# Soft MoE on one core: dispatch weights turned in 32-squares by VectorE, gathered in four row groups; down products of two experts in column halves; maxima spread by DRAM

## The chip, the cores and the metric

The kernel runs on one core of a Trainium2 chip. The metric is the device time of one execution in microseconds (us), lower being better. The core has five engines that run side by side: PE (TensorE, matrix products; PEld is its loading of weights), DVE (VectorE), ACT (ScalarE), POOL (GpSimd) and SP (SyncE, which issues DMAs here). SBUF is the on-chip memory, PSUM holds PE's results, DRAM is the memory off the core.

## The reference, cut to what matters

Two layers of linear attention and a soft mixture of experts, then a second block of two layers with another attention and a gated network; residuals are added after each. The change concerns the mixture alone:

```python
x = layernorm(x)                       # 8 batches, 256 tokens, 128 features
se = layernorm(slot_embeds) * scale    # 16 experts x 64 slots, 128 features
logits = einsum('bnd,esd->bnes', x, se)
dispatch = softmax(logits, axis=1)     # over the tokens
combine = softmax(logits.reshape(b, n, -1), axis=-1)   # over all 1024 slots
slots = einsum('bnd,bnes->besd', x, dispatch)
gate = gelu(einsum('besd,edf->besf', slots, Wg) + bg)
up = einsum('besd,edf->besf', slots, Wu) + bu
eout = einsum('besf,efo->beso', gate * up, Wd) + bd
return einsum('bns,bso->bno', combine, eout.reshape(b, -1, 128))
```

All of it is in fp32. The mixture runs in two layers, so 8 batches make 16 dispatches, and 16 experts make 8 pairs in each of 2 layers and 2 groups of batches, 32 pairs in all.

## The kernel before

The eight batches form two groups of four. A group goes through both mixture layers (the linear attention follows each batch's first combine), then the gated networks and the second attention. The whole program is written as steps for a planner: a step names the engines that can run it with a cost in ns each, the function that issues its instructions, and what it reads, writes and takes as buffers. The planner places steps one after another, always the one that can start earliest by its costs, with ties broken by a key that grows with PE's work; the second group's key starts 45000 later. Each engine then gets its instructions in the order of planned starts, by hand. So PE fills a wait of one group with steps of the other, and a changed cost changes the order of everything. Buffers are counted by kind (`kinds`: `comb`, `k4`, `we`, `ps` and others), and a step waits for a free one in the plan too; `ps` is PSUM's eight banks.

`dispatch(b, sl)` works on one batch. `norm` gives the rows `y` (tokens on partitions, two tiles of 128), `transposed` gives `yt`. Four steps `logits` (L511) form the logits with slots on partitions, two blocks of 128 slots each, which `evacuated` copies into `comb`. Then two paths leave `comb`.

- The dispatch softmax, by halves of four slot blocks: `greatest` (L542, DVE), `exps` (L550, ACT, into `ex`), `inverse` (L558, DVE), `divided` (L563, POOL). The result has slots on partitions, while the gather contracts over tokens, so `turn` flips it in PE, 8 flips of 128x128 a half (all flips have the line L331), each four evacuated from PSUM into `dm` (L338 on ACT or L340 on DVE). `gathered` (L584) multiplies `y` with `dm`, 512 columns at a time, and `affinely` (L416 or L418) scales the slots into `sl`.
- The combine softmax: `greater` (L528, DVE) keeps running maxima over the slot blocks, `fold` (L603, DVE) joins two halves, `turn_max` flips them (L331), `token_max` (L614, DVE) gives one maximum a token, and `spread` (L623, PE, two products with a broadcast operand) puts them on all partitions. `less` (L635, POOL) subtracts them and `exps` (L641, ACT) finishes `comb`, which is first read in `combine` (L742, PE), after the experts.

`experts(sl)` runs over 16 experts. `fetch` loads the expert's weights and its down bias into one of three `we` buffers (SP, L660 and L661). `front` makes gate and up products (L675, 256 columns: four batches of 64 slots), a gelu (L681, ACT) and the product with up (L686, DVE), giving `ht`. `back` makes the down products (L705, PE) of one expert: two batches' slots stand on 128 output partitions, and `biased` (L715, DVE) adds the bias in two instructions of 64 partitions, into the place in `sl` that the expert's slots had. For that the copies in `sl` and the embeddings `seT` have an order of halves that depends on whether the batch is odd; a third copy in `seT` (L464, POOL) serves this.

Two places elsewhere already use PE in tiles: `projected` in the second attention (L1131, four groups of 32 rows) and `products` there (L1223, four groups of 32 columns). L1027, L1030 and L958 are the gated network's products; L972 is a DVE addition there of a 128x512 PSUM tile and an SBUF tile.

Of the kernel before, what the change touches and what calls it, by code (L numbers as in the profile page):

```python
# [13 lines left out]
P = 128  # L14
# [162 lines left out]
def macaron_kernel(ctx: ExitStack, tc: tile.TileContext, i: dict, out: bass.AP):  # L177
# [27 lines left out]
        "comb": (NJ * N, 9),  # L205
        "slots": (NJ * NB * 4 * S1, G),
        "k4": (1024, 6),
# [3 lines left out]
        "we": (6 * P + D, 3),  # L211
# [98 lines left out]
    seT = const.tile([P, NJ, 3, S], F32, tag="seT", name="seT")  # L310
# [11 lines left out]
    def mms(*columns):  # L322
        return sum(2 * max(107, 0.84 * n) for n in columns)
# [24 lines left out]
    def normalized(tiles, twice=False):  # L348
# [21 lines left out]
        step({"DVE": 400 * n}, stats, [t[2] for t in tiles], [mv], takes=[t[3] for t in tiles])  # L370
        step({"POOL": 600 + 160 * n}, root, [mv], [mv])
        for t, (dst, src, r, w) in enumerate(tiles):
            def apply(e, t=t, dst=dst, src=src):
                (nc.gpsimd if e == "POOL" else nc.vector).tensor_scalar(  # L374
                    dst(), src(), mv.ap[:, 2 * t : 2 * t + 1], mv.ap[:, 2 * t + 1 : 2 * t + 2],
                    ALU.subtract, ALU.mult,
                )

            step({"POOL": 800, "DVE": 360}, apply, [r, mv], [w])
# [31 lines left out]
    def affinely(dst, src, r, w, n):  # L411
# [8 lines left out]
        step({"ACT": act(n, True), "DVE": dve(n, 120)}, run, [*r, "ng"], w)  # L420


    def keys():
# [8 lines left out]
        for h in range(2):  # L432
# [17 lines left out]
            def finish(e, pse=pse, part=part):  # L450
                if e == "ACT":
                    nc.scalar.activation(
                        seT[:, part, 0:2], pse.ap, AF.Identity, bias=bs, scale=gs
                    )
                else:
                    nc.vector.tensor_scalar(
                        seT[:, part, 0:2], pse.ap, gs, bs, ALU.mult, ALU.add
                    )
# [3 lines left out]

            def again(_, part=part):
                nc.gpsimd.tensor_copy(seT[:, part, 2], seT[:, part, 0])  # L464

            step({"POOL": 400}, again, cells, [("seT2", j) for j in js])
# [25 lines left out]

    def dispatch(b, sl):


        odd, q = b % 2, b % BG
        y = norm(b, True)
        yt = transposed(y, TT, True)
        comb = Buf("comb", (P, NJ, N))
        pm = Buf("k2", (P, 2, N))
        for u in range(4):
            pl = ps_(2, N)

            def logits(_, u=u, pl=pl):
                for j in range(2):  # L510
                    mm(  # L511
                        pl.ap[:, j, :],
                        seT[:, 2 * u + j, odd : odd + 2].rearrange("p k s -> p (k s)"),
# [5 lines left out]
                [yt, *((k, 2 * u + j) for j in range(2) for k in ("seT", "seT2"))], [pl],  # L519
                takes=[(comb, u), pm],  # L520
# [5 lines left out]
            if u:  # L526
                def greater(_, u=u, pl=pl):
                    nc.vector.tensor_tensor(  # L528
                        pm.ap, pl.ap, comb.ap[:, 0:2, :] if u == 1 else pm.ap, ALU.max
                    )  # L530

                step({"DVE": dve(2 * N)}, greater, [pl, pm, (comb, 0)], [pm])


        for h in range(2):
            mx = Buf("sm", (P, 16))
            ex = Buf("k4", (P, 4, N))
            dm = Buf("k4", (P, TT, 4 * P))
            half = [(comb, 2 * h), (comb, 2 * h + 1)]

            def greatest(_, h=h, mx=mx):
                nc.vector.tensor_reduce(  # L542
                    mx.ap[:, 0:4], comb.ap[:, 4 * h : 4 * h + 4, :], AX.X, ALU.max, negate=True
# [4 lines left out]
            def exps(_, h=h, mx=mx, ex=ex):  # L548
                for j in range(4):
                    nc.scalar.activation(  # L550
                        ex.ap[:, j, :], comb.ap[:, 4 * h + j, :], AF.Exp,
# [3 lines left out]
            step({"ACT": 2200}, exps, [*half, mx], [mx, ex], [dm], table="exp")  # L555
# [6 lines left out]
            def divided(_, mx=mx, ex=ex):  # L562
                nc.gpsimd.tensor_tensor(  # L563
                    ex.ap, ex.ap, mx.ap[:, 8:12].unsqueeze(2).to_broadcast([P, 4, N]), ALU.mult
                )

            step({"POOL": 1950}, divided, [mx, ex], [ex])
            for t in range(TT):
                pt = ps_(4, P)

                def turn(_, t=t, pt=pt, ex=ex):
                    for j in range(4):
                        flip(pt.ap[:, j, :], ex.ap[:, j, ts(t, P)])

                step({"PE": flips(4)}, turn, [ex], [pt], takes=[dm])
                evacuated(
                    lambda t=t, dm=dm: dm.ap[:, t, :],
                    lambda pt=pt: pt.ap.rearrange("p j c -> p (j c)"), [pt], [(dm, t)], 4 * P,
                )
            po = ps_(4, 2, S)  # L580

            def gathered(_, dm=dm, po=po):
                for t in range(TT):
                    mm(  # L584
                        po.ap.rearrange("p j k s -> p (j k s)"), y.ap[:, t, :], dm.ap[:, t, :],
                        start=(t == 0), stop=(t == TT - 1),
                    )

            step(
                {"PE": mms(512, 512)}, gathered,  # L590
                [(y, t) for t in range(TT)] + [(dm, t) for t in range(TT)], [po],
            )


            blocks = slice(1, 3) if odd else slice(0, 4, 3)
            affinely(
                lambda h=h: sl.ap[:, 4 * h : 4 * h + 4, q // 2, blocks, 0:S],
                lambda po=po: po.ap, [po], [(sl, j, q) for j in range(4 * h, 4 * h + 4)], 512,
            )


        def fold(_):
            nc.vector.tensor_tensor(pm.ap[:, 0], pm.ap[:, 0], pm.ap[:, 1], ALU.max)  # L603

        step({"DVE": dve(2 * N)}, fold, [pm], [pm])
# [3 lines left out]
        def turn_max(_):  # L609
            for t in range(TT):  # L610
                flip(pt.ap[:, t, :], pm.ap[:, 0, ts(t, P)])
# [6 lines left out]
        pb = ps_(N)  # L618
        mb = Buf("k1", (P, N))

        def spread(_):
            for t in range(TT):
                mm(  # L623
                    pb.ap[:, ts(t, P)], mn.ap[:, t : t + 1].to_broadcast([P, P]), ident,
                    start=True, stop=True,
                )

        step({"PE": mms(P, P)}, spread, [mn], [pb], takes=[mb])
        evacuated(lambda: mb.ap, lambda: pb.ap, [pb], [mb], N)
# [17 lines left out]
    def experts(sl):  # L647
        def whole(j):
            return [(sl, j, q) for q in range(BG)]

        def eo():
            return sl.ap.rearrange("p j a k s -> p j (a k s)").rearrange(
# [3 lines left out]
        def fetch(e):  # L656
            we = Buf("we", (P, 6 * P + D))

            def run(_):
                nc.sync.dma_start(we.ap[:, 0 : 6 * P], i["We"][e])  # L660
                nc.sync.dma_start(we.ap[:, 6 * P :], i["bd"][e].partition_broadcast(P))  # L661

            step({"SP": 1000}, run, [(sl, 0, BG - 2)], [we])
            return we

        def front(e, we):
            j, k = e // 2, e % 2
            ht = Buf("k2", (P, 2, BG * S))
            for c in range(2):
# [3 lines left out]
                def hidden(_, c=c, pe=pe):  # L673
                    for m in range(2):
                        mm(  # L675
                            pe.ap[:, m, :], we.ap[:, ts(2 * m + c, P)],
                            sl.ap[:, j, :, k::2, 0:S], start=True, stop=True,
# [7 lines left out]
                def up(_, c=c, pe=pe, ga=ga):  # L685
# [6 lines left out]
                    {"PE": mms(256, 256)}, hidden, [we, *whole(j)], [pe], takes=[ga, (ht, c)]  # L692
# [5 lines left out]
        def back(e, we, ht):  # L698
            j, k = e // 2, e % 2
            po = ps_(NB, P)  # L700

            def down(_):
                for q in range(NB):
                    for c in range(2):
                        mm(  # L705
                            po.ap[:, q, :], ht.ap[:, c, ts(q, P)], we.ap[:, ts(4 + c, P)],
                            start=(c == 0), stop=(c == 1),
                        )

            step({"PE": mms(*[P] * 2 * NB)}, down, [we, (ht, 0), (ht, 1)], [po])  # L710

            def biased(_):
                for u in range(2):
                    rows = slice(u * S, (u + 1) * S)
                    nc.vector.tensor_tensor(  # L715
                        eo()[rows, j, (u ^ k) :: 2, 0:D], po.ap[rows],
# [624 lines left out]
```

## Time and profile before

| what | value |
|---|---|
| median of 3 runs | 789.29 us (788.82 to 789.86) |
| profiled execution, its own time | 788.46 us |
| its span | 786.8 us |
| PE busy | 759.1 us, 96% |
| DVE busy | 536.7 us, 68% |
| ACT busy | 458.3 us, 58% |
| POOL busy | 340.6 us, 43% |
| DMA, mean over the span | 47 GB/s |

Busy times come from one profiled execution. The span is from its first to its last instruction; the execution's own time is 1.7 us longer. A group of instructions is shown as its line, engine and operation, what it writes and reads by the program's names, its shape and its count, then busy time, mean ns of one, and after the second bar the engine's idle time before them with what ended it. A single fp32 product shows as two records, a flip as one. A record's duration is longer than the distance from one record to the next[...]; distances are read from the order of time.

### The profile page before, as it was taken

To read this page: it belongs to the slowest core of one execution; us is meant where nothing else is said; L and a number is where in the kernel's file an instruction comes from. 1 tells how busy PE (TensorE), PEld (TensorE's weight loads), DVE (VectorE), ACT (ScalarE), POOL (GpSimd) and SP (SyncE) were. 2 spreads that over 40 slices of the span, in tenths; PEclk is the share of its full clock that TensorE was granted. 3 is DMA by queue.
4 is the path that set the end of the run, shared out by engine and by line. 5 is a ranking of instruction groups with operands and counts; after the bars stand their busy time and mean duration, and the time that the engine had idled before them with its cause. 6 is when DMAs were issued, how large, how long until landed. Compare 5 with 4: busy or idle time off the path is not lost.

```text
span 786.8 us, 12435 instructions
## 1 busy us (share of the span) xinstructions
PE 759.1 (96%) x4584; PEld 630.9 (80%) x4584; DVE 536.7 (68%) x1170; ACT 458.3 (58%) x826; POOL 340.6 (43%) x365
## 2 busy tenths in 40 slices
PE   3899999999999999999999999999999999999997
PEld 2667787999887888878888987898787987778875
DVE  5899787478886887895664455447897488873242
ACT  2889889555894689895363324426475255633232
POOL 7998424323367545547722042234544323620001
PEclk9999999999999999999999999999999999999999
DMA  6101233313230122332523100000000000000000
GB/s 192 40 0 39 77 97 95 112 54 114 74 95 1 55 66 76 94 106 58 153 74 92 47 1 1 1 0 2 1 1 1 1 1 15 2 0 1 21 7 15
DMA packets 27580, 36.96 MB, mean 47 GB/s; under 512 B 3808, under 2 KB 18816, under 8 KB 27520
## 3 DMA queue, kind: packets, MB, share of 16 engines
q1 hardware_dynamic: 25968, 35.62, 15.4%
q8 instruction: 36, 0.59, 0.3%
q10 hardware_dynamic: 1488, 0.53, 0.3%
q14 instruction: 24, 0.20, 0.1%
q0 software_dynamic: 64, 0.03, 0.0%
HBM read 35.12 MB, written 1.05 MB: 46 GB/s over the span
## 4 chain that ended last, share of the span: by engine, by line
PE 87%; DVE 5%; POOL 4%; DMA 1%; issue 1%; ACT 1%; ACTq 0%; POOLq 0%; SPq 0%; DVEq 0%
PE ps L958 24%; PE ps L675 13%; PE ps L742 7%; PE ps L705 7%; PE ps L331 5%; PE ps L511 5%; PE ps L584 5%; PE ps L1030 4%; PE ps L1055 3%; PE ps L1027 3%; PE ps L1192 2%; POOL k L563 1%; PE ps L1131 1%; PE ps L1117 1%; PE ps L1223 1%; POOL sm L368 1%
## 5 line engine op out<-in xcount | busy, mean ns | idle before, releaser
L675 PE MATMUL ps<-slots,we 128*128 128x256 f32 x512 | 124.4, 380 | 0.0
L338 ACT COPY k<-ps 128x512 f32<-128x512 f32 (+1 forms) x97 | 50.5, 540 | 122.1 <-PE ps L958 74.3
L675 PEld LDWEIGHTS ps<-slots,we 128*128 128x128 f32 x512 | 93.0, 189 | 17.6 <-issue 6.0
L958 PE MATMUL ps<-comb,comb 128*128 128x256 f32 x448 | 104.6, 381 | 2.5 <-ACT k L338 1.7
L958 PE MATMUL ps<-comb,slots 128*128 128x256 f32 x448 | 103.4, 379 | 0.0
L563 POOL TENSOR_TENSOR k<-k,sm 128x1024 f32<-128x1024 f32 x32 | 61.0, 1908 | 85.8 <-DVE sm L558 85.7
L958 PEld LDWEIGHTS ps<-comb,comb 128*128 128x128 f32 x448 | 83.3, 190 | 16.2 <-ACT k L338 2.7
L958 PEld LDWEIGHTS ps<-comb,slots 128*128 128x128 f32 x448 | 83.9, 190 | 14.3 <-issue 3.6
L635 POOL TENSOR_TENSOR comb<-comb,k 128x1024 f32<-128x1024 f32 x32 | 75.8, 2386 | 19.4 <-DVE k L340 14.1
L681 ACT ACTIVATE k<-ps,bg 128x256 f32<-128x256 f32 x128 | 55.3, 473 | 41.3 <-PE ps L675 36.2
L331 PE MATMUL ps<-ident,k 128*128 128x128 f32 x408 | 61.7, 279 | 16.5 <-POOL k L374 9.1
L686 DVE SCALAR_TENSOR_TENSOR k<-ps,bu,k 128x256 f32<-128x256 f32 x128 | 56.9, 477 | 25.1 <-ACT k L681 24.2
L972 DVE TENSOR_TENSOR comb<-ps,k 128x512 f32<-128x512 f32 x48 | 33.0, 688 | 59.5 <-ACT k L338 30.1
L331 PEld LDWEIGHTS ps<-ident,k 128*128 128x128 f32 x408 | 48.8, 143 | 28.6 <-POOL k L374 10.9
L705 PEld LDWEIGHTS ps<-we,k 128*128 128x128 f32 x512 | 65.0, 191 | 7.5 <-issue 3.4
L715 DVE TENSOR_TENSOR slots<-ps,we 64x256 f32<-64x256 f32 x128 | 53.7, 420 | 25.0 <-PE ps L705 20.0
L705 PE MATMUL ps<-we,k 128*128 128x128 f32 x512 | 67.6, 275 | 0.8 <-DVE k L686 0.8
L550 ACT ACTIVATE k<-comb,sm 128x256 f32<-128x256 f32 x128 | 63.4, 498 | 5.8 <-DVE sm L542 3.4
L943 POOL TENSOR_TENSOR comb<-comb 128x512 f32<-128x512 f32 x16 | 25.1, 1570 | 92.8 <-ACT comb L980 56.2
L511 PE MATMUL ps<-k,seT 128*128 128x256 f32 x256 | 62.7, 384 | 0.7 <-ACT k L416 0.7
L742 PEld LDWEIGHTS ps<-slots,comb 128*128 128x128 f32 x512 | 59.6, 192 | 3.0 <-issue 2.6
L742 PE MATMUL ps<-slots,comb 128*128 128x129 f32 x512 | 60.8, 275 | 0.0
(143 smaller groups left out, 1413.1 us busy)
## 6 DMA issues: line engine op xcount, KB each, us to landing
we<-in_We SPq DMA_DIRECT2D x64, 384.0 KB, 3.1
we<-in_bd SPq DMA_DIRECT2D x64, 64.0 KB, 3.0
x<-in_L_attn_x SPq DMA_DIRECT2D x4, 256.0 KB, 5.9
comb<-in_h2T SPq DMA_DIRECT2D x4, 256.0 KB, 4.6
slots<-in_h1T SPq DMA_DIRECT2D x4, 256.0 KB, 6.3
out<-x SPq DMA_DIRECT2D x8, 128.0 KB, 1.7
k<-in_slot_embeds ACTq DMA_DIRECT2D x2, 256.0 KB, 6.1
k<-in_hs SPq DMA_DIRECT2D x2, 256.0 KB, 3.5
```

The costliest lines, as they stand in the source:

```text
L331: nc.tensor.transpose(po, src, ident)
L511: mm(pl.ap[:, j, :], seT[:, 2 * u + j, odd : odd + 2].rearrange("p k s -> p (k s)"), yt.ap, start=True, stop=True,)
L550: nc.scalar.activation(ex.ap[:, j, :], comb.ap[:, 4 * h + j, :], AF.Exp, bias=mx.ap[:, j : j + 1], accum_out=mx.ap[:, 4 + j : 5 + j],)
L563: nc.gpsimd.tensor_tensor(ex.ap, ex.ap, mx.ap[:, 8:12].unsqueeze(2).to_broadcast([P, 4, N]), ALU.mult)
L635: nc.gpsimd.tensor_tensor(raw, raw, mb.ap.unsqueeze(1).to_broadcast([P, 4, N]), ALU.subtract)
L675: mm(pe.ap[:, m, :], we.ap[:, ts(2 * m + c, P)], sl.ap[:, j, :, k::2, 0:S], start=True, stop=True,)
L681: nc.scalar.activation(ga.ap, pe.ap[:, 0, :], AF.Gelu, bias=bg[:, e, c : c + 1])
L686: nc.vector.scalar_tensor_tensor(ht.ap[:, c, :], pe.ap[:, 1, :], bu[:, e, c : c + 1], ga.ap, ALU.add, ALU.mult,)
L705: mm(po.ap[:, q, :], ht.ap[:, c, ts(q, P)], we.ap[:, ts(4 + c, P)], start=(c == 0), stop=(c == 1),)
L715: nc.vector.tensor_tensor(eo()[rows, j, (u ^ k) :: 2, 0:D], po.ap[rows], we.ap[rows, 6 * P :].unsqueeze(1).to_broadcast([S, NB, D]), ALU.add,)
L742: mm(po.ap[:, t, 0 : D + 1], comb.ap[:, j, ts(t, P)], eo()[:, j, q, 0 : D + 1], start=(j == 0), stop=(j == NJ - 1),)
L958: mm(bank.ap[:, o], w(k)[:, c, ts(o, P)], rhs().rearrange("p (c n) -> p c n", c=2)[:, c, :], start=(start and o + c == 0), stop=(stop and ...
```

## The change

- Dispatch weights: `turn` is now a DVE transpose of 128x1024 a half, in place, which turns every square of 32x32 by itself. Slots of a square stand on its 32 columns and 32 tokens on its partitions; each group of 32 partitions then holds 32 of every 128 slots, for all 256 tokens in eight chunks. `ex` is now one buffer of kind `comb` for both halves; `dm` and its evacuations are gone.
- Rows: each group of 32 partitions needs all tokens, so `replicated` writes `y` to DRAM in four DMAs and reads it back in four, once for each group of partitions, as `yr`.
- Gather: for each of eight chunks four products of 32 rows and 256 columns, one in each row group of PE, each into its own PSUM bank; then four affine copies of 256 columns.
- Maxima: `largest` is one DVE reduction of 128x2048 over the slot blocks (its eight neighbours lie 256 elements apart). `spread` on PE becomes a DMA of the two columns of maxima to DRAM and one that reads them back to all partitions.
- Experts: `back` does a pair. Each expert's down product has 64 columns of weights and goes to one column half of PE, and so to 64 of the output's partitions; one DVE addition of 128x512 adds the bias. The odd and even orders of halves, and the third copy in `seT`, are gone. The pair's two weight buffers are held to the end of its down product.
- Buffers: `comb` 9 to 10, `k4` 6 to 4, `we` 3 to 4.
- The planner's costs of several steps are set anew.

```diff
-        "comb": (NJ * N, 9),
+        "comb": (NJ * N, 10),
-        "k4": (1024, 6),
+        "k4": (1024, 4),
-        "we": (6 * P + D, 3),
+        "we": (6 * P + D, 4),
...
-        return sum(2 * max(107, 0.84 * n) for n in columns)
+        return sum(2 * max(112, 0.84 * n) for n in columns)
...
-        step({"DVE": 400 * n}, stats, [t[2] for t in tiles], [mv], takes=[t[3] for t in tiles])
+        step({"DVE": 455 * n}, stats, [t[2] for t in tiles], [mv], takes=[t[3] for t in tiles])
-            step({"POOL": 800, "DVE": 360}, apply, [r, mv], [w])
+            step({"POOL": 840, "DVE": 430}, apply, [r, mv], [w])
-        step({"ACT": act(n, True), "DVE": dve(n, 120)}, run, [*r, "ng"], w)
+        step({"ACT": act(n, True) + 90, "DVE": dve(n, 120)}, run, [*r, "ng"], w)
...
+        def spill(_):
+            for k in range(4):
+                nc.sync.dma_start(
+                    spilled[b].rearrange("i (t k) d -> i k t d", k=4)[:, k],
+                    y.ap[32 * k : 32 * k + 32],
+                )
+        def spread(_):
+            for a in range(4):
+                nc.sync.dma_start(yr.ap[32 * a : 32 * a + 32], spilled[b])
+        step({"SP": 1800}, spill, [(y, t) for t in range(TT)], [("y", b)])
+        step({"SP": 1800}, spread, [("y", b)], [yr])
...
-                    nc.vector.tensor_tensor(
-                        pm.ap, pl.ap, comb.ap[:, 0:2, :] if u == 1 else pm.ap, ALU.max
-                    )
...
-                def turn(_, t=t, pt=pt, ex=ex):
-                    for j in range(4):
-                        flip(pt.ap[:, j, :], ex.ap[:, j, ts(t, P)])
...
+                nc.vector.transpose(
+                    ex.ap[:, part].rearrange("p j n -> p (j n)"),
+                    ex.ap[:, part].rearrange("p j n -> p (j n)"),
+                )
+            step({"DVE": 1200}, turn, [(ex, h)], [(ex, h)])
...
-                for t in range(TT):
-                    mm(
-                        po.ap.rearrange("p j k s -> p (j k s)"), y.ap[:, t, :], dm.ap[:, t, :],
-                        start=(t == 0), stop=(t == TT - 1),
-                    )
+            for c in range(N // 32):
+                for a, po in enumerate(pos):
+                    rows = slice(32 * a, 32 * a + 32)
+                    mm(
+                        po.ap, yr.ap[rows, c, :], ex.ap[rows, :, 32 * c : 32 * c + 32],
+                        start=(c == 0), stop=(c == N // 32 - 1), tile_position=(32 * a, 0),
+                    )
+        step({"PE": 3600}, gathered, [yr, (ex, 0), (ex, 1)], pos)
...
-            nc.vector.tensor_tensor(pm.ap[:, 0], pm.ap[:, 0], pm.ap[:, 1], ALU.max)
+            nc.vector.tensor_reduce(
+                pm.ap, comb.ap.rearrange("p j n -> p n j"), AX.X, ALU.max
+            )
...
-                mm(
-                    pb.ap[:, ts(t, P)], mn.ap[:, t : t + 1].to_broadcast([P, P]), ident,
-                    start=True, stop=True,
-                )
+            nc.sync.dma_start(maxima[b].rearrange("t p -> p t"), mn.ap)
+            nc.sync.dma_start(
+                mb.ap, maxima[b].rearrange("t p -> (t p)").partition_broadcast(P)
+            )
...
-            step({"SP": 1000}, run, [(sl, 0, BG - 2)], [we])
+            step({"SP": 1000}, run, [(sl, "in", BG - 2, 0)], [we])
...
-                    {"PE": mms(256, 256)}, hidden, [we, *whole(j)], [pe], takes=[ga, (ht, c)]
+                    {"PE": mms(256, 256)}, hidden, [we, *whole(j), *filled], [pe], takes=[ga, (ht, c)]
...
-                        mm(
-                            po.ap[:, q, :], ht.ap[:, c, ts(q, P)], we.ap[:, ts(4 + c, P)],
-                            start=(c == 0), stop=(c == 1),
-                        )
+                        for k in range(2):
+                            mm(
+                                po.ap[S * k : S * k + S, q, :], hts[k].ap[:, c, ts(q, S)],
+                                wes[k].ap[:, ts(4 + c, P)], start=(c == 0), stop=(c == 1),
+                                tile_position=(0, S * k),
+                            )
...
-                        eo()[rows, j, (u ^ k) :: 2, 0:D], po.ap[rows],
-                        we.ap[rows, 6 * P :].unsqueeze(1).to_broadcast([S, NB, D]), ALU.add,
+                    eo()[:, j, :, 0:D], po.ap,
+                    wes[0].ap[:, 6 * P :].unsqueeze(1).to_broadcast([P, BG, D]), ALU.add,
...
-            if e >= 1:
-                back(e - 1, *got.pop(e - 1))
+            if e % 2 == 0 and e:
+                back(e // 2 - 1, *zip(*got[e - 2 : e]))
+        back(NJ - 1, *zip(*got[E - 2 :]))
...
-        step({"DVE": 500}, blocks, [pkv], [kv])
+        step({"DVE": 730}, blocks, [pkv], [kv])
...
-            step({"POOL": 1200, "DVE": 800}, run, r, w)
+            step({"POOL": 1450, "DVE": 950}, run, r, w)
```

## The prediction

> **What bounds the kernel now.** I read the page's busy shares, then the chain that ended last, then a table of stretches, then the costliest groups, and last the order of TensorE's work in two short windows.
>
> ```profile
> PE 759.1 (96%) x4584; PEld 630.9 (80%) x4584; DVE 536.7 (68%) x1170; ACT 458.3 (58%) x826; POOL 340.6 (43%) x365
> PE 87%; DVE 5%; POOL 4%; DMA 1%; issue 1%; ACT 1%; ACTq 0%; POOLq 0%; SPq 0%; DVEq 0%
> ```
>
> PE is busy for 96% of the span and carries 87% of the chain. A busy PE needn't be a full one, so I look at start distances: in the order of PE's work a 128-column record starts 0.11 us after the one before it, a 256-column one after 0.216, a 512-column one after 0.43. All records times these distances make 743 us of 786.8. PE's own work sets the time.
>
> ```profile
> 15.00:66.00 51.00, 47.27 (x228) 35.15 (x229) 45.78 (x86) 43.40 (x118) 50.32 (x42) 1.00 0.09 29
> 66.00:200.00 134.00, 132.47 (x822) 114.51 (x821) 102.41 (x248) 98.98 (x175) 52.70 (x63) 1.00 0.30 87
> 200.00:350.00 150.00, 147.93 (x896) 125.05 (x895) 122.56 (x276) 121.92 (x255) 79.64 (x74) 1.00 0.24 71
> 400.00:787.00 387.00, 379.49 (x2330) 313.75 (x2329) 228.66 (x450) 165.32 (x236) 111.05 (x122) 1.00 0.04 13
> ```
>
> Columns: stretch, length, busy time of PE, PEld, DVE, ACT, POOL, clock, DMA share, GB/s. From 66 us on PE alone is full. The opening (15 to 66, before the first expert) is different: POOL is busy 50.3 of 51 us, DVE 45.8, ACT 43.4. There a shorter PE buys nothing by itself.
>
> ```profile
> L331 PE MATMUL ps<-ident,k 128*128 128x128 f32 x408 | 61.7, 279 | 16.5 <-POOL k L374 9.1 <-DVE k L374 4.3 <-POOL k L563 1.9
> L584 PE MATMUL ps<-k,k 128*128 128x512 f32 x128 | 60.3, 593 | 0.0
> L705 PE MATMUL ps<-we,k 128*128 128x128 f32 x512 | 67.6, 275 | 0.8 <-DVE k L686 0.8
> L623 PE MATMUL ps<-ident,sm 128*128 128x128 f32 x64 | 9.8, 276 | 0.4 <-DVE sm L614 0.4
> ```
>
> These are the PE groups that the edit touches: flips, the gather of slots, the down products, the spreading of maxima.[...]
>
> ```profile
> 38.56 1.04 PE L331 MATMUL ps<-ident,k 128*128 128x128 f32 x8
> 39.44 1.89 PE L511 MATMUL ps<-k,seT 128*128 128x256 f32 x8
> ...
> 553.06 1.02 PE L1027 MATMUL ps<-k,w1T 128*128 128x512 f32 x2
> 554.01 1.07 PE L1223 MATMUL ps<-k,kv 128*32 128x256 f32 x16
> 555.01 1.12 PE L1030 MATMUL ps<-k,w2T 128*128 128x512 f32 x2
> ```
>
> Start, length, group. Eight flips take 39.44 - 38.56 = 0.88 us, 0.110 each. L1223 is an existing product on four column tiles: 16 records of 256 columns in 1.00 us, where one after another they would take 16 x 0.216 = 3.46. So tiles do run side by side, four at a time.
>
> [...]L1223 gets 3.46/1.00, and L1131 (four row groups, 32 records of 128 columns) takes 1.10 us where 3.6 would be serial. [...]L1027's two records need 0.86 us but L1223 starts 0.95 after them, and its own four rounds of 0.216 last 1.00, so a burst pays about 0.09 on the way in and 0.13 inside and out, 0.22; L1131's, by the same count, 0.3.
>
> **PE, part by part.** There are 16 dispatches (8 batches, 2 layers) and 32 expert pairs.
> - Flips of dispatch weights go: 16 x 16 x 0.110 = 28.2 us off.
> - The spread by PE goes: 64 records x 0.112 = 7.2 off.
> - Gather: before, 128 records x 0.43 = 55.0. After, 8 chunks x 4 row groups of 256 columns, two records each: 16 rounds x 0.216 = 3.46 a dispatch, 55.3 in all. Four row groups only make up for contracting 32 rows at a time. Plus 16 bursts x 0.22 = 3.5.
> - Down products: before, 512 x 0.112 = 57.3. After, twice the products with half the columns of weights, two tiles side by side: 16 rounds x 0.112 a pair, again 57.3. Plus 32 bursts x 0.25 (between the two measured) = 8.0.
>
> Sum: -28.2 - 7.2 + 0.3 + 3.5 + 8.0 = **-23.6 us** of PE time.
>
> **What the opening gives back.** In 15 to 66 us some 60 of those flips and all of 16 spread records run: 6.6 + 1.8 = 8.4 us, less about 0.8 for three or four new bursts, 7.6. POOL's two passes a half (L563 1.91, L635 2.39 us) stay, so POOL, DVE and ACT keep the opening at its length and PE waits there. I count **+7.6**. It could be 0: the subtraction L635 (19.3 us of POOL in the opening) will come later, behind the DMAs, so that L563 goes first and the experts may start sooner. Late next would be DVE.
>
> **VectorE.** Removed: running maxima L528 32.7 us (21.7 + 11.0), L603 12.6, the 128 bias adds L715 53.7, and about half of 64 evacuations of flipped weights, 19. Added: 32 transposes of 128x1024. None is in the trace;[...] I take L542, a pass over the same 128x1024, 1.21 us: 39 us; twice that is the upper end[...]. 16 maxima over a view whose neighbours lie 1 KB apart: 2.2 us if like L542,[...] 35 is the lower end. 32 bias adds of 128x512 by L972's 0.69: 22. Affine copies: 64 of 256 columns in place of 32 of 512 (0.53 against 0.81 on DVE, 0.56 against 0.78 on ACT): up to +10, on either.[...] DVE's 537 us has 250 to spare; from 66 us on PE hides all of it. In the opening the same counts leave DVE and ACT about where they are. ACT loses some 18 us of evacuations.
>
> **Waits and queues.** The rows y go to DRAM and come back four times over: eight DMAs, two landings of about 3 us (We lands in 3.1). In the first dispatch the gather starts 13 us after y, so 6 us are hidden. Maxima: two DMAs, 2.9 us as norm_g's 128 single words and 3.0 as the broadcast bo, in place of 0.85 us on PE and ACT. L635 waits for that, and behind it only L641 and the combine at L742, first at 146 us while the dispatches' L635 end near 84: 60 us of cover. All ten DMAs join SP, in front of weight fetches: each dispatch holds SP for two landings. SP already waits 215 us for L705 to free weight buffers, so it is idle time that they fill; bounds 0 to 32 x 2 us, taken 0. The weights of two experts are now held until the pair's down product; a fetch then has only the next expert's 1.8 us of PE in front of it against 3.1 us to land: 1.3 us short, 28 times. Before, the same sum is 3.1 against 1.8 + 0.9, 0.4 short, and PE shows no wait for it: the other group's work fills it. Taken 0, bound 36. Two fewer copies on POOL (L464): 0.8, under the opening's start. The gather now takes four PSUM banks and starts for all eight slot blocks at once, so the first expert waits for whole dispatches, not halves: inside the opening's +7.6. Bias DMAs are as many and half as large: 0.
>
> The new planner costs reorder everything. PE lies idle 12.1 us in all after 66 us; a better order saves at most that, a worse one may double it. I take 0.
>
> **Sum.** -23.6 + 7.6 = -16.0 on an execution of 788.46 us (span 786.8 and 1.7 around it); the median shown is 0.8 above it: 789.29 - 16 = **773 us**.
>
> **Rivals.**
> - The whole PE gain arrives, because the experts start sooner: 766; with half of the idle time planned away, 760. For it: L635 leaves the head of POOL's queue. Against: DVE is busy 90% of the opening. Chance 0.22.
> - Slower: the weights of pairs. If the 28 short fetches, with SP held by landings in front of them (up to 2 us more), are not filled by the other group, each costs 1.3 to 2 us: up to 36 to 56 us, 809 at 36. It decides from 16 us of stall, 0.6 us a pair. Against: PE is full from 66 us on with a similar shortage now. With half of it, 791. Chance 0.16.
> - In between, some of that stall: 780 to 789, chance 0.09, of which 0.04 is no change.
> - The tiles don't do what they say: half-width column tiles run one after another, +57 us, 830. L1223 with quarter tiles speaks against it. Chance 0.02, inside the slower ones.
>
> **Numbers.** The forecast, 769 to 779, has 0.53. Faster by over 0.2% (1.6 us, about what a measurement here can tell) 0.80; within 0.04; slower 0.16. Range 757 (whole gain and most idle time) to 794 (a bit over half of the fetch stall).
>
> **What would show it.** Right: L331's records drop by 256 to 152 plus the 64 others, L623 is gone, gather records of 256 columns start in fours 0.216 us apart, down records in pairs 0.11 apart; PE's idle time grows by about 8 us before the first expert and not after. Wrong: waits of PE for DMA into we, a first expert well away from 66 us, transposes over 2 us that make DVE the releaser of PE, or down records that start singly.

## The result, and the profile after

The changed kernel takes **909.2 us** (904.2 to 910.5, four runs) against 789.1 for the kernel before: the ratio is 1.151 [1.147, 1.156]. I had forecast 773. The profiled execution took 910.47 us, span 908.8, so the two spans differ by 122.0 us.

I read the same views again, first the busy shares and the chain that ended last.

```profile
PE 776.4 (85%) x5672; PEld 646.5 (71%) x5672; DVE 526.1 (58%) x1018; ACT 441.0 (49%) x808; POOL 342.1 (38%) x365
PE 61%; DMA 19%; POOL 7%; DVE 6%; ACT 3%; issue 3%; SPq 1%; ACTq 0%; POOLq 0%
```

PE carries 61% of the chain where it carried 87%, and DMA 19% where it had 1%. PE's idle time (span less busy) grew from 27.7 to 132.4 us, by 104.7; its busy time grew by 17.3. Together that is the 122.0. Then the stretches, with the columns of before:

```profile
15.00:66.00 51.00, 31.82 (x220) 26.26 (x221) 35.33 (x49) 26.51 (x78) 26.62 (x27) 0.80 0.53 77
66.00:200.00 134.00, 95.67 (x836) 78.61 (x838) 73.01 (x108) 76.38 (x154) 53.36 (x37) 0.86 0.31 84
200.00:350.00 150.00, 122.90 (x1048) 108.76 (x1040) 93.40 (x195) 76.62 (x157) 53.20 (x63) 0.92 0.22 67
...
500.00:909.00 409.00, 401.00 (x2532) 326.87 (x2531) 223.62 (x442) 179.26 (x256) 130.61 (x142) 1.00 0.05 16
```

No engine is full in any of the first three stretches, which have the dispatches: in the first, PE is busy 31.8 of 51 us, POOL 26.6 (50.3 before). So no single engine's work sets the time there, and the chain names DMAs. From 500 us on, where no dispatch is left, PE is full as before. The granted clock (third column from the right) falls to 0.80; it was 1.00 everywhere. In this trace it is 1.00 or 0.50 at any moment, and the column is the mean over the stretch. The first expert starts at 102.3 us, where it started at 65.6: with PE's waits for weights below, that makes two of the signs of being wrong that the prediction had named.

The groups that the edit touched:

```profile
L596 PE MATMUL ps<-comb,k 32*128 32x256 f32 x1024 | 67.5, 416 | 17.5 <-ACT k L416 12.5 <-ACT comb L562 3.1 <-DVE sm L775 1.3
L724 PE MATMUL ps<-we,k 128*64 128x128 f32 x1024 | 66.7, 283 | 4.7 <-DVE k L704 4.7
L612 DVE TENSOR_REDUCE k<-comb 128x256 f32<-128x2048 f32 x16 | 58.9, 3679 | 0.0
L583 DVE STREAM_TRANSPOSE comb<-comb 128x1024 f32<-128x1024 f32 x32 | 39.4, 1236 | 48.6 <-POOL comb L575 47.9
L646 POOL TENSOR_TENSOR comb<-comb,k 128x1024 f32<-128x1024 f32 x32 | 74.5, 2350 | 135.9 <-DMA k<-m 131.3
L331 PE MATMUL ps<-ident,k 128*128 128x128 f32 x152 | 28.7, 296 | 38.3 <-DVE k L612 17.8 <-POOL k L374 11.5 <-ACT slots L416 5.0
```

The transposes cost 1.236 us each (1.21 estimated, as L542), the strided maxima 3.68 (2.2 if like L542). L646 is the subtraction of the maxima. In the kernel before it was this:

```profile
L635 POOL TENSOR_TENSOR comb<-comb,k 128x1024 f32<-128x1024 f32 x32 | 75.8, 2386 | 19.4 <-DVE k L340 14.1 <-ACT k L338 5.2
```

Each pass is as long as ever (2.35 us for 2.39), but POOL now stands idle 131.3 us in front of it for the maxima's read. Two bursts in the order of PE's work show the tiles:

```profile
278.17 3.73 PE L596 MATMUL ps<-comb,k 32*128 32x256 f32 x64
...
291.63 2.02 PE L724 MATMUL ps<-we,k 128*64 128x128 f32 x32
293.58 1.13 PE L693 MATMUL ps<-slots,we 128*128 128x256 f32 x4
```

A gather burst has 64 records of 256 columns: 13.8 us one after another, 3.7 here. A pair's down burst has 32 of 128 columns: 3.6 us one after another, 293.58 - 291.63 = 1.95 here. Tiles run four and two at a time, as forecast.

Now the queue that issues the DMAs. L632 is the store of the maxima, L635 their read:

```profile
78.98 0.38 SPq L632 DMA_DIRECT2D m<-sm  x1
88.31 0.34 SPq L635 DMA_DIRECT2D k<-m  x1
89.04 0.37 SPq L632 DMA_DIRECT2D m<-sm  x1
99.22 0.33 SPq L635 DMA_DIRECT2D k<-m  x1
104.90 0.37 SPq L632 DMA_DIRECT2D m<-sm  x1
113.79 0.32 SPq L635 DMA_DIRECT2D k<-m  x1
114.20 3.53 SPq L673 DMA_DIRECT2D we<-in_We  x2
```

These lines stand one after another. In 35 us SP issues three stores of 1 KB and their three reads and nothing else, in the order of its program: each read waits for its store to land, and comes 9.0, 9.8 and 8.5 us after the store's issue has ended. The weights (L673) come after that. The DMA issues of the page (KB each, median us from issue to landing), and the waits (us in total, times, longest):

```profile
we<-in_We SPq DMA_DIRECT2D x64, 384.0 KB, 4.4
y<-k SPq DMA_DIRECT2D x64, 32.0 KB, 1.9
k<-m SPq DMA_DIRECT2D x16, 128.0 KB, 4.8
...
m<-sm SPq DMA_DIRECT2D x16, 1.0 KB, 9.1
```

```profile
POOL comb L646 <- DMA k<-m: 131.3, 14, 17.8
PE ps L693 <- DMA we<-in_We: 25.9, 11, 6.0
PE ps L763 <- POOL slots L744: 24.1, 4, 10.3
SPq L635 <- DMA m<-sm: 108.6, 15, 9.8
```

The store of 1 KB takes 9.1 us to land, a store of 32 KB of rows 1.9. SP stands 108.6 us for it in 15 waits. PE waits for weights, and for a memset (L744) that is behind the subtraction on POOL (one at 194.3 us stands behind a subtraction that waited until 186.0 for its maxima). How POOL's order carries the wait on, from its timeline (the bracket is idle time before the group):

```profile
32.12 1.59 POOL L374 TENSOR_SCALAR k<-x,sm 128x128 f32<-128x128 f32 x2
48.67 4.65 POOL L646 TENSOR_TENSOR comb<-comb,k 128x1024 f32<-128x1024 f32 x2 [14.96 <-DMA k<-m]
53.28 5.59 POOL L575 TENSOR_TENSOR comb<-comb,sm 128x1024 f32<-128x1024 f32 x3
```

POOL stands 15 us and then has three divisions of dispatch weights (L575) to catch up. The turns on DVE (L583, 47.9 us of idle time behind L575) and the gather after them wait for those.

### The profile page after: what moved, and what is told of

Same layout as the page of the kernel before. It is cut to its first block, busy times and chain, and to the rows that moved or that the text cites. A ratio compares the mean times of both kernels' runs of the same rounds, so it can differ in the third digit from the quotient of the medians.

```text
span 908.8 us, 14628 instructions
## 1 busy us (share of the span) xinstructions
PE 776.4 (85%) x5672; PEld 646.5 (71%) x5672; DVE 526.1 (58%) x1018; ACT 441.0 (49%) x808; POOL 342.1 (38%) x365
## 4 chain that ended last, share of the span: by engine, by line
PE 61%; DMA 19%; POOL 7%; DVE 6%; ACT 3%; issue 3%; SPq 1%; ACTq 0%; POOLq 0%
PE ps L979 21%; PE ps L693 10%; DMA m<-sm 8%; PE ps L724 5%; DMA k<-m 5%; DMA we<-in_We 4%; POOL comb L646 4%; PE ps L763 4%; PE ps L1076 3%; PE ps L1051 3%; PE ps L1048 3%; PE ps L528 2%; PE ps L331 2%; DVE k L612 2%; PE ps L1213 2%
## 5 line engine op out<-in xcount | busy, mean ns | idle before, releaser
L693 PE MATMUL ps<-slots,we 128*128 128x256 f32 x512 | 134.5, 407 | 27.6 <-DMA we<-in_We 25.9
L646 POOL TENSOR_TENSOR comb<-comb,k 128x1024 f32<-128x1024 f32 x32 | 74.5, 2350 | 135.9 <-DMA k<-m 131.3
L763 PE MATMUL ps<-slots,comb 128*128 128x129 f32 x512 | 68.8, 292 | 24.1 <-POOL slots L744 24.1
L338 ACT COPY k<-ps 128x512 f32<-128x512 f32 (+1 forms) x63 | 32.9, 528 | 115.1 <-PE ps L979 71.8
L652 ACT ACTIVATE comb<-comb 128x1024 f32<-128x1024 f32 x32 | 33.8, 1055 | 103.4 <-POOL comb L646 98.3
L575 POOL TENSOR_TENSOR comb<-comb,sm 128x1024 f32<-128x1024 f32 x32 | 60.2, 1895 | 62.0 <-DVE sm L570 62.0
L704 DVE SCALAR_TENSOR_TENSOR k<-ps,bu,k 128x256 f32<-128x256 f32 x128 | 57.5, 476 | 44.0 <-ACT k L699 43.7
L596 PE MATMUL ps<-comb,k 32*128 32x256 f32 x1024 | 67.5, 416 | 17.5 <-ACT k L416 12.5
L596 PEld LDWEIGHTS ps<-comb,k 32*128 32x128 f32 x1024 | 57.8, 207 | 25.3 <-ACT comb L338 12.7
L724 PE MATMUL ps<-we,k 128*64 128x128 f32 x1024 | 66.7, 283 | 4.7 <-DVE k L704 4.7
L724 PEld LDWEIGHTS ps<-we,k 128*64 128x64 f32 x1024 | 58.2, 141 | 15.8 <-DVE k L704 7.1
L583 DVE STREAM_TRANSPOSE comb<-comb 128x1024 f32<-128x1024 f32 x32 | 39.4, 1236 | 48.6 <-POOL comb L575 47.9
```

The lines of the kernel that those rows point to most:

```text
L575: nc.gpsimd.tensor_tensor(ex.ap[:, part], ex.ap[:, part], mx.ap[:, 8:12].unsqueeze(2).to_broadcast([P, 4, N]), ALU.mult,)
L583: nc.vector.transpose(ex.ap[:, part].rearrange("p j n -> p (j n)"), ex.ap[:, part].rearrange("p j n -> p (j n)"),)
L596: mm(po.ap, yr.ap[rows, c, :], ex.ap[rows, :, 32 * c : 32 * c + 32], start=(c == 0), stop=(c == N // 32 - 1), tile_position=(32 * a, 0),)
L646: nc.gpsimd.tensor_tensor(raw, raw, mb.ap.unsqueeze(1).to_broadcast([P, 4, N]), ALU.subtract)
L652: nc.scalar.activation(raw, raw, AF.Exp)
L693: mm(pe.ap[:, m, :], we.ap[:, ts(2 * m + c, P)], sl.ap[:, j, k, :, 0:S], start=True, stop=True,)
```

## The experiments

Theory A: the stores of the maxima, by SP and POOL standing in order behind them, make the 120 us. Rivals: the pairs of experts (B), the dispatch part (B2), the strided maxima on DVE (C), the new planner costs.

**The maxima's way: PE again, and DMAs alone.** In the changed kernel, the maxima are spread by PE as before:

```diff
-        step({"SP": 450}, spill, [mn], [("max", b)])
-        step({"SP": 450}, spread, [("max", b)], [mb])
+        step({"PE": mms(P, P)}, spread, [mn], [pb], takes=[mb])
+        evacuated(lambda: mb.ap, lambda: pb.ap, [pb], [mb], N)
```

> The changed kernel, with the maxima spread by two PE products and an evacuation again, as before the change; all else is the changed kernel. Theory A (the two DMAs of the maxima, 9.1 and 4.8 us to landing where the plan counts 2.65 each, hold SP's and POOL's queues in order): the loss goes, and the PE sum of the prediction shows: 789 - 23.6 + 7.2 + 7.6 = 780, at most 790. Theory B (the weights of pairs held longer, rows by eight DMAs and the four-bank gather make the loss): 870 or more.

Measured: 812.2 us, ratio to before 1.031 [1.028, 1.034]. 97 us of the 120 are gone. It is not the 780 expected, so something else costs too. The opening and the next stretch of this run:

```profile
15.00:66.00 51.00, 43.65 (x328) 37.07 (x330) 46.54 (x60) 39.58 (x114) 45.12 (x36) 0.93 0.41 116
66.00:200.00 134.00, 124.09 (x1117) 106.24 (x1113) 93.72 (x178) 83.91 (x152) 49.78 (x54) 0.97 0.27 85
```

All engines are back at work, still short of before (47.3 and 132.5 of PE). The counterpart is the kernel before with nothing but the two DMAs in place of PE's spread:

> The kernel before, with one part of the change alone: maxima spread by the two DMAs in place of two PE products and an evacuation. Theory A: much slower, 840 to 900, with POOL waiting for the reading DMA by over 80 us in all. Theory B: within 2% of before, 780 to 800.

Measured: 889.5 us, 1.128 [1.126, 1.129], 101 us slower, with no rows through DRAM, no tiles and no pairs. Its store lands in 9.1 us as well, and POOL waits 122.5 us for the read. A holds in both directions.

**Is it the form of the store?** The changed kernel, with the two columns of maxima flipped by PE into two rows first, so that the store writes two rows of 512 B in place of 256 single words:

```diff
+            flip(prow.ap[0:TT, :], mn.ap)
...
+            nc.vector.tensor_copy(mrow.ap[0:TT, :], prow.ap[0:TT, :])
...
-            nc.sync.dma_start(maxima[b].rearrange("t p -> p t"), mn.ap)
+            nc.sync.dma_start(maxima[b], mrow.ap[0:TT, :])
```

> The changed kernel; the maxima (two words on each of 128 partitions) are first flipped by PE to two rows of 128 words and copied by DVE, so that the store to DRAM is two runs of 512 B and not 256 single words; the reading DMA is unchanged. Theory A1 (single words stored to DRAM are what takes 9 us): the store lands in 2 to 2.5 us, as the rows y do (1.9), and the time falls to 775 to 795. Theory A2 (any way through DRAM that the queues wait for costs it): the store still lands late, or the time stays over 850.

Measured: 833.6 us, 1.057 [1.054, 1.060]: 76 us less than the changed kernel, though not the 775 to 795 expected. The waits:

```profile
POOL comb L656 <- DMA k<-m: 75.1, 13, 17.6
SPq L643 <- DMA m<-k: 10.3, 10, 2.0
```

SP's wait for the store falls from 108.6 us to 10.3: between the end of a store's issue and its read lie 7.1 to 10.2 us with single words, and with rows SP never stands longer than 2.0 for a store. POOL still waits 75 us for the read, which comes in SP's turn; yet the time is only 21 us above that of the kernel with PE's spread, so a total of waits is not a price.

**Is it the plan?** The planner had been told 0.45 us for each of the two DMAs and a lag of 2.2 us for all DMAs (from a step's end until its successor may start). With lags by the trace:

```diff
-            s.ready = max((n.end + self.LAG[n.engine] for n in s.needs), default=0)
+            s.ready = max((n.end + getattr(n, "lag", self.LAG[n.engine]) for n in s.needs), default=0)
...
-        step({"SP": 450}, spill, [mn], [("max", b)])
-        step({"SP": 450}, spread, [("max", b)], [mb])
+        step({"SP": 450}, spill, [mn], [("max", b)]).lag = 8700
+        step({"SP": 450}, spread, [("max", b)], [mb]).lag = 4400
```

> The changed kernel with the same instructions; the planner alone is told that the store of the maxima takes 8.7 us from its issue until its successor may start, and the reading DMA 4.4, where it counted 2.2 for both. Theory A-plan (the queues are put in an order that the real times don't fit, and would do no harm in a fitting one): most of the loss goes, 775 to 810. Theory A-wait (SP standing at the landing is the loss whatever the order): over 870.

Measured: 859.6 us, 1.092 [1.087, 1.097], between the two. A plan that knows the delay wins back 50 us: it puts other work ahead of the subtraction, and POOL's wait for the read falls from 131.3 to 43.9 us. It doesn't take the stores off SP: they take 11.7 us to land here, and PE waits 38.5 us for weights.

**SP or POOL?** The same stores and reads, but nobody waits for them on POOL:

```diff
-                    raw, raw, mb.ap.unsqueeze(1).to_broadcast([P, 4, N]), ALU.subtract
+                    raw.rearrange("p j (t c) -> p (j t) c", c=P),
+                    raw.rearrange("p j (t c) -> p (j t) c", c=P),
+                    ident.unsqueeze(1).to_broadcast([P, 4 * TT, P]), ALU.subtract,
...
-            step({"POOL": 2400}, less, [mb, *half], half)
+            step({"POOL": 2400}, less, half, half)
```

> The changed kernel with both DMAs of the maxima still issued on SP, in the same form, but nobody reads what they bring: the subtraction on POOL takes the identity in place of the maxima (same shape and engine, and the exponent a scale of 0.125, so the combine weights are not the reference's) and waits for no DMA. The changed kernel with the maxima on PE took 812 us, 97 less than the changed kernel. Theory POOL: the 97 us come from POOL standing in order behind the subtraction that waits for the maxima (131 us of waits). Then this run falls to 800 to 830. Theory SP: they come from the 9.1 us stores that hold SP, so that rows and weights are fetched late. Then it stays at 870 or above, with PE's waits for the DMA into we at some 26 us as before. In between, both.

Measured: 866.5 us, 1.099 [1.096, 1.102], between the ranges of the two theories, so both have a share. Of the 97 us 43 go with POOL's wait, 54 stay with the stores on SP. The split is rough, since the plan's order moves with the edit, and the two are not independent: PE's wait for weights grows to 49.8 us here. Waits of this run:

```profile
PE ps L695 <- DMA we<-in_We: 49.8, 10, 18.1
...
SPq L635 <- DMA m<-sm: 105.2, 14, 9.3
```

SP stands as long as in the changed kernel (108.6 there); the weights of the experts come up to 18 us late, and PE waits for them.

**The strided maxima (C).** Running maxima of the kernel before in place of L612, in the kernel with PE's spread:

> The changed kernel with the maxima spread by PE (812 us in the run before) and, on top, with the running maxima and the fold of the kernel before in place of the one strided reduction of 128x2048, which takes 3.68 us where the plan counts 2.30. Theory C (that reduction stands on DVE in front of the work that PE waits for): 12 us or more faster than 812. Theory B (weights of pairs, rows through DRAM): no more than 5 us faster.

Measured: 822.8 us, 1.043 [1.042, 1.045], 10 us more than with the strided reduction. C falls.

**The new costs.** The kernel before with only the planner's six changed costs:

> The kernel before with the new planner costs alone: the same instructions in another order. The prediction took 0 for this, with 12 us of PE's idle time as the bound: 782 to 801. If the new costs fit the chip better, as their sizes suggest (128 columns 112 against 107 ns, statistics 455 against 400), 782 to 788; a theory that the new order itself makes the rest of the loss: 800 or more.

Measured: 791.9 us, 1.0039 [1.0024, 1.0054]: 3 us.

**The experts alone.** The kernel before with pairs, column halves, the order of `sl` and four weight buffers:

> The kernel before with the experts' part of the change alone: down products of two experts in column halves, one bias addition for both, four weight buffers, the plain order of halves; dispatch, maxima and planner costs are those of before. By the burst times of the run before (1.90 us a pair against 1.79) PE's sum gives 788.5 + 32 x 0.2 = 795 if nothing waits. Theory B1 (the weights of a pair held longer are what costs): 805 to 825, with PE waiting for DMA into we. Against B1: 788 to 797.

Measured: 809.7 us, 1.026 [1.025, 1.028], 21 us. The time lies in the range of the theory, but PE waits for weights only 3.5 us in all, so the stall that I had made the slower rival is not there. To part holding from tiles, this run has full-width products, but holds two experts' weights and puts their `back` steps together:

```diff
-            if e >= 1:
-                back(e - 1, *got.pop(e - 1))
+            if e % 2 == 0 and e:
+                back(e - 2, *got.pop(e - 2))
+                back(e - 1, *got.pop(e - 1))
```

> The kernel before with one thing of the pairs: four weight buffers (and 12 for 14 of the smallest temporaries, to make room), and the down products and bias adds of two experts issued together after both fronts, still full width, one expert after the other, without tiles. The pairs alone cost 21 us. Theory hold: the price is in holding the weights of two experts and in the order that this makes: 800 to 806, PE's busy time as before. Theory tiles: the price is in the tiles themselves, in the 32 bursts[...]: 787 to 792.

Measured: 797.5 us, 1.011 [1.010, 1.013], between the two: 9 us for holding. The bursts make 32 x 0.20 = 6.4. No run tells the last 6 of 21 apart. In the trace of the experts alone PE is idle 7 us longer than before (808.1 - 773.3 = 34.8 us for 27.7), and the mean granted clock is 0.994, which costs at most 808.1 x 0.006 = 4.8 (an estimate); with the bursts that is 18 of the 21.

**The dispatch part alone.** DVE's turns, rows through DRAM and the gather in row groups, with PE's spread, running maxima and the old experts and costs:

> The kernel before with the dispatch part of the change alone: weights turned by VectorE, rows through DRAM, gather in four row groups; maxima (running, spread by PE), experts and planner costs are those of before. PE's sum: 788.5 - 27.9 + 16 x 0.33 = 766, and 773 with the opening's give-back of the prediction. Theory B2 (rows through DRAM and the four-bank gather cost it): 785 to 805. Against B2: 764 to 777.

Measured: 792.4 us, 1.0047 [1.0031, 1.0063]. PE's sum for this part is 28.2 less 0.3 and some 5 for 16 bursts, near 23 us, so 766; 26 us are given back. Two of its stretches, with the columns of before:

```profile
15.00:66.00 51.00, 42.52 (x260) 33.37 (x259) 45.83 (x78) 40.29 (x117) 45.95 (x42) 0.87 0.22 61
...
200.00:350.00 150.00, 141.41 (x1128) 126.21 (x1127) 125.65 (x284) 110.84 (x241) 77.67 (x77) 0.99 0.33 93
```

I took the opening for the place, and kept PE's flips in its four dispatches (with `comb` and `k4` at the 9 and 6 of before, and the planner's offset of the second group at 52 us):

> The kernel before with the dispatch weights turned by VectorE and gathered in four row groups in 12 of the 16 dispatches; the first four, those of the opening, keep PE's flips and its gather of 512 columns. The planner's offset of the second half of the batches is 52 us in place of 45. The 12 spare PE 12 x (1.76 - 0.33) = 17 us. Theory opening: what all sixteen gained (23 us of PE) was given back in the opening, which DVE, POOL and ACT bound; with the opening left alone 774 to 783, stretch 15 to 66 as before with PE busy about 47 us and at a full clock. Rival: a turned dispatch gives its gain back wherever it stands, by DVE's turns, the rows' way through DRAM and the order: 787 to 796.

Measured: 798.9 us, 1.012 [1.010, 1.014], above both ranges. Its stretches:

```profile
15.00:66.00 51.00, 48.77 (x233) 37.13 (x234) 46.72 (x88) 43.59 (x116) 50.32 (x43) 1.00 0.21 55
...
200.00:350.00 150.00, 138.05 (x1100) 123.13 (x1099) 131.25 (x277) 108.38 (x231) 72.94 (x72) 0.98 0.32 90
```

The opening is whole again, and yet PE is busy 138 us in 200 to 350 where it was busy 148 before. So the opening is not the only place; as offset and buffers moved too, this run can't say what the opening alone is worth. Another offset for all sixteen:

> All sixteen dispatches turned by VectorE and gathered in row groups, nothing else of the change, as in the run that took 792.4 us, but with the planner's offset of the second half of the batches at 48 us in place of 45. Theory order: the gain of 23 us of PE was lost to an unlucky order, which the offset moves: 780 to 786. Theory opening: the opening takes it back under any such order: 789 to 796, with PE busy 42 to 44 us in 15 to 66 at a low clock.

Measured: 789.8 us, 1.0010 [0.9998, 1.0022], no difference from before. This other order doesn't bring the gain, and the result lies in the range of the opening's theory, with the signs named for it: PE is busy 42.5 of 51 us in 15 to 66, at a clock of 0.90. Then I took one suspect at a time, with the order of all engines kept. Without the DVE transposes:

> The dispatch part alone (792.4 us) with its 32 DVE transposes left out, so that the slots are gathered with wrong weights; their place in the plan and its cost stay, so the order of every engine is the same. 39 us of DVE are gone. Theory turns: the 22 us that PE saves are lost because DVE's turns stand in front of the gather and of DVE's other work: 772 to 782. Theory rows: little, 789 to 793. Theory order and stages (the opening's other engines, the plan's own order): 786 to 793.

Without the stores of the rows, and so without waits for their landing:

> The dispatch part alone with the rows y not written to DRAM: the four reads take the same number of bytes of the input in place of them, so the slots are gathered from wrong rows, and no read waits for a store's landing. 64 stores and 16 landings are gone from SP, the order of the rest is the same. Theory rows: 775 to 785. Theory turns: 789 to 793. Theory order and stages: 787 to 793.

Without either:

> The dispatch part alone with both left out, DVE's transposes and the stores of the rows. What this run still stands above 788.5 minus 22 = 766 us is neither DVE's turning nor the rows' way: under 772 the two explain all of it; at 785 or above the order and the stages' other engines do.

Measured: 787.1 (0.998 [0.997, 0.999]), 784.6 (0.995 [0.993, 0.996]) and 778.2 us (0.988 [0.986, 0.989]). Against the 792.4 of the whole dispatch part, DVE's turns cost 5 us on the path, the rows' stores and landings 8, both 14 of the 26. The other 12 lie in neither. The trace of the run without either shows where up to 9 of these are: in the opening. PE is idle 8.2 us there for 3.7 before, and the granted clock is 0.90 there for 1.00, which costs at most 42.8 us of busy time x 0.10 = 4.3 (an estimate). The last run was meant to beat both kernels: rows from SBUF to SBUF, no landing to wait for, but 16 DMAs a dispatch in place of 8 (both branches of the `if` name SP):

```diff
-                nc.sync.dma_start(yr.ap[32 * a : 32 * a + 32], spilled[b])
+                for k in range(4):
+                    (nc.sync if k % 2 else nc.sync).dma_start(
+                        yr.ap[32 * a : 32 * a + 32].rearrange("i (t k) d -> i k t d", k=4)[:, k],
+                        y.ap[32 * k : 32 * k + 32],
+                    )
```

> The dispatch part alone with the rows moved from SBUF to SBUF in 16 DMAs a dispatch, without DRAM: SP issues 16 x 0.6 = 10 us a dispatch in place of 8 x 0.6 and one landing of 2 us, but no DMA waits for another. If the rows' price (8 us, as the run without stores shows) is the landing that holds SP, 784 to 787, and this beats both kernels. If it is the time that SP spends on issuing, it grows: 794 to 810, with PE waiting for DMA into we.

Measured: 836.4 us, 1.059 [1.056, 1.061], slower even than the 794 to 810 of SP's issuing. From SP's timeline, and the waits:

```profile
14.30 42.88 SPq L506 DMA_DIRECT2D k<-k  x64
57.23 0.58 SPq L684 DMA_DIRECT2D we<-in_We  x1
```

```profile
PE ps L699 <- DMA we<-in_We: 36.2, 10, 9.6
```

SP issues 64 of these in 42.9 us, 0.67 each, with no wait between, and the first weights come after. The run has 128 more DMAs to issue than the dispatch part with rows by DRAM, none of them waits for a landing, and it is 44 us slower. No version that I ran with the whole computation is faster than the kernel before.

## Why the prediction was wrong, point by point

- **PE's sum, right.** The records times their start distances fall from 742.8 to 708.0 us, by 34.8; I had 28.2 + 7.2 - 0.3 = 35.1. A gather burst loses 0.31 (0.22 taken): at the whole clock it starts 0.09 us late, and 3.67 us pass from its first record to the next product's, where 3.46 would do. A pair's burst loses 0.20 (0.25 taken). That is +11.4 against +11.5. The rival that tiles don't run side by side is out.
- **DVE's transposes, right,** to 3% (1.236 us for 1.21), and DVE did not become the bound: its busy time fell from 536.7 to 526.1 us. For the strided maxima the traces of before gave only the 2.2 us of a pass like L542; my higher price was an estimate that none of them showed. They take 3.68 us, 58.9 in all.
- **"Maxima: two DMAs, 2.9 us as norm_g's 128 single words": the step that failed first.** I priced a store of 256 words to DRAM by a load of 128 words, and by the cheaper of two such loads in the view of before:

```profile
norm_g<-in_norm_g SPq DMA_DIRECT2D x1, 0.5 KB, 2.9
...
norm_b<-in_norm_b SPq DMA_DIRECT2D x1, 0.5 KB, 5.1
```

The store takes 9.1 us, the read 4.8 for 3.0 taken. That SP waits so little for the row form (10.3 us in `after_row`, for 108.6) shows that the form of the store is the cause: 256 pieces of 4 B hold SP for up to 9.8 us at a time, two of 512 B for up to 2.0. The runs don't part the size of the pieces from their number, and show nothing of how.
- **"It is idle time that they fill; bounds 0 to 32 x 2 us, taken 0": the step that failed in size.** SP's waits before were for weight buffers, ahead of time:

```profile
SPq L660 <- PE ps L705: 215.0, 46, 56.2
```

They are no free time: what a wait holds up is what comes next in SP's order, and that was weights and rows which PE needed soon. With 9.1 us a store SP stood 108.6 us. `after_free` leaves 54 us for this, and `direct16` shows that SP's own issuing, without any landing, can hold the weights up too (PE waits 36.2 us for them).
- **"Behind it only L641 and the combine": failed.** I looked for the readers of the maxima and found 60 us of cover. Behind the subtraction on POOL stand the next dispatch's division (L575), the norms' passes (L374) and the experts' memsets (L744). Without POOL's wait for the maxima (`after_free`) the time is 43 us shorter.
- **The pairs: waits taken 0, bound 36; measured 21 with the bursts.** The bound held. The mechanism did not: PE waits 3.5 us for weights, and 9 us come with the two experts' steps put together.
- **The opening's +7.6: about right, but not all.** With the dispatch part alone (`gather`) PE is idle 8.5 us of the opening where it was idle 3.7 (one wait of 5.0 us is for the running maxima on DVE), and the granted clock there is 0.87 for 1.00, which costs at most 42.5 us of busy time x 0.13 = 5.5 (an estimate): up to 10.3 us together. But that part gave back 26 us, and some of it later: in 200 to 350 us PE is idle 8.6 us for 2.1. Left out, DVE's turns give 5 us and the rows' stores 8. I had both at nothing: the waits on SP "taken 0", and for DVE "PE hides all of it".
- **Clock, not in the sum at all.** PE's busy time grew by 17.3 us though its work fell by 34.8 - 11.4 = 23.4. Of the 41 us between them the trace gives 34 to the granted clock: it is 0.50 in 15 stretches, 112.6 us in all, PE is busy in 68.7 of these, and its 256-column products there start 0.427 us apart in place of 0.216, so half of the 68.7 is the price. The account of the 122.0 us is then: 104.7 more of idle time, 34 by the clock, less 23.4 of work; 6 are left over.
- **Parts.** Alone they cost 101 us (maxima), 21 (pairs), 4 (dispatch) and 3 (costs), 129 in sum; together 120. Without the maxima by DRAM my sum would have been -9 and the chip shows +24: the sign would have been wrong too.

## What to carry to other kernels

Price a DMA by one that has its direction, its piece and its number of pieces: here 256 single words out to DRAM took 9.1 us where 128 words in had taken 2.9 and 5.1. And before you put a DMA on a queue or a wait in front of an instruction, list what stands behind it on that engine, on SP as well: a full engine hides nothing for the queue that feeds it. A saving on the busiest engine arrives only as far as all its feeders keep up; try each part by itself before adding the parts.

## What the runs showed of the hardware that I had not expected

- A store of 256 single words took 9.1 us to land (median) in two kernels (the changed one and `before_dram`) and 11.7 in `after_lag`; stores of 32 KB in rows took 1.9. For the same 1 KB as two rows SP stood at most 2.0 us at a time (`after_row`).
- The granted clock was lower where PE was idle more, on a single core: 1.00 throughout with PE idle 27.7 us of the span (`before`), 0.93 in the opening of the kernel with PE's spread (PE busy 43.7 of 51 us), 0.80 in that of the changed kernel (31.8 of 51). In the trace of the changed kernel it is 1.00 or 0.50 and never between, and the 15 stretches at 0.50 last from 3.41 to 17.07 us. PE had been busy for at most 41% of the 3.41 us before 14 of them; the last, at 704.8 us, came with PE busy throughout. As I read it, idle time came in twice: 104.7 us by itself, and most of the 34 in the records at the lower clock after it.
- SP spent 0.67 us on each of 64 DMAs of 32 KB between parts of SBUF (`direct16`), one after another, with no wait between them.
